# Self attentions of a four-layer decoder: value products regrouped into four 32-column blocks, results gathered by selecting matmuls, TensorE kept in written order

## The chip, the cores and the metric

The kernel runs on one core of one Trainium2 chip. The metric is the device time of the whole program in microseconds (us). Three runs of the kernel before took 5355.73, 5357.63 and 5362.43 us; the median is 5357.63 us. About 0.2% (some 11 us) is what a measurement of this kernel can tell from no change.

## The reference, cut to what matters

The model is a decoder of four layers on 16 batches of 100 tokens with 128 features, all in float32. Each layer is a self attention, a cross attention to 1444 context rows and a feed-forward part, each with a residual. Only the four self attentions are changed. All have 16 heads of 8 features (q, k), and 100 queries against 100 keys:

```python
# layer 0 (scores / 0.1, values times a gate), layer 1 (plain), both causal
scores = where(causal, einsum('bhqd,bhkd->bhqk', q, k) * scale, -inf)
out = einsum('bhqk,bhkd->bhqd', softmax(scores), v) ; x += out @ w_out.T
# layer 2, not causal: two attention maps over values of 16 features per head
att = softmax(q1 @ k1) - lam * softmax(q2 @ k2)
y = einsum('bhts,bhse->bhte', att, v); y = rmsnorm(y) * ... ; x += y @ c_w.T
# layer 3, causal: q and k normed, scores clipped before the softmax
scores = where(causal, clip(q @ k * scale, -5, 5), -10000); attn = softmax(scores / 1.5)
```

## The kernel before, in words

`run` calls twelve stages one after the other; each begins with a layer norm of `X` (100 tokens on the partitions, 16 batches x 128 features), so a stage can't begin before the one before it has written its last batch of `X`. The stages that the change touches are `l0_attn`, `l1_attn`, `l2_attn` and `l3_attn`.

A self attention first norms and turns `X`, then projects `qT` and `kT` (features on the partitions, `project`) and values per batch (`ps_v`) into `va`, a tile of 9 columns per head: 8 values and a column of ones, whose product gives the softmax's sum (17 columns in layer 2). Then it loops over units: one batch in layers 0, 1 and 3, and one batch of one of the two maps in layer 2, so 16, 16, 32 and 16 units. One unit is:

- `attn_scores`: GpSimd spreads the keys into `kb` (each head's 8 rows kept, the others zero, L287). Four matmuls of 400 columns (L298) give the scores of 16 heads in PSUM. VectorE adds the mask or clips (L305, L307), or VectorE and ScalarE copy (L311), into `sc`. VectorE takes the row maxima `mx` (L313), GpSimd subtracts them (L314), ScalarE takes the exponential (L315).
- `attn_pv`: 16 transposes (L328) in four groups of four, each group into one of two PSUM banks of `psT`, evacuated by `copy`, which takes VectorE and ScalarE in turn (L247, L249). Then 16 matmuls (L333), one per head: the turned numerators are the weights (100x100) and 9 or 17 columns of values move. VectorE takes the reciprocal of the sums, `rs` (L335).
- `o` (L419) is the normed result; `attn_out` turns it (`ps_ot`, L344), copies it (`ot`, L346), multiplies it with the output weights (`ps_out`, L349) and adds it to `X` (L351). In layer 2 this comes after the loop, for 16 batches.

The scores of unit b+1 are written ahead of the transposes of unit b. The order on each engine is not the written one: a planner orders the instructions of each engine by when it reckons them ready, with the written order as priority. An instruction that goes through `tc.keep_in_program_order` is tied behind the one written before it on its engine. `l0_xattn` and `l2_xattn` tie all their matmuls in this way; the self attentions tie none. [...] in a self attention `psS` has two tiles of two banks, `psT` two of one, `psO` two of one. Every float32 matmul appears in the trace as two weight loads and two passes.

`l2_xattn` already multiplies values in the way that the change brings to the self attentions: 32 value columns as weights, four such blocks side by side in TensorE's columns (`ps_O`, L1018), then four matmuls with a constant of zeros and ones, `so`, that pick the heads' columns out (`ps_o`, L1051).

Of the kernel before, what the change touches and what calls it, by code (L numbers as in the profile page):

```python
# [9 lines left out]
F32 = mybir.dt.float32  # L10
U8 = mybir.dt.uint8
AF = mybir.ActivationFunctionType
# [20 lines left out]
def _pack(parts, axis):  # L33

    at, n = {}, 0
    for name, a in parts:
        at[name] = (n, a.shape[axis])
        n += a.shape[axis]
    return np.ascontiguousarray(np.concatenate([a for _, a in parts], axis=axis)), at


def _layout(i):
# [54 lines left out]
        ("ident", (p == q)), ("hmask", p // 8 == np.arange(NH)[None, :]), ("tri", tri), ("tri3", tri3),  # L97
# [50 lines left out]
    hm, so = np.zeros((4, 32, 4), f), np.zeros((4, 32, 4, NH, 9), f)  # L148
    uk, uv = up(i["L2_xattn_wk"], i["L2_xattn_bk"]), up(i["L2_xattn_wv"], i["L2_xattn_bv"])
    for r in range(4):  # L150
        for a in range(4):
            blk, o, h = (0, 9 * a, 3 * r + a) if a < 3 else (1, 0, 12 + r)
            d = slice(8 * h, 8 * h + 8)
            qa[:, blk, r, o : o + 8] = i["L2_xattn_wq"][:, d]
            qb[32 * r + o : 32 * r + o + 8, blk, 0] = i["L2_xattn_bq"][d]
            ka[:, blk, r, o : o + 8], va[:, blk, r, o : o + 8] = uk[:, d], uv[:, d]
            ka[CD, blk, r, o + 8] = va[CD, blk, r, o + 8] = 1.0
            hm[r, o : o + 8, a], hm[r, o + 8, a] = 1.0 / math.sqrt(8.0), 1.0
            so[r, o + np.arange(9), a, h, np.arange(9)] = 1.0
    arr["l2x"], xat["l2x"] = _pack([  # L160
        ("q", qa.reshape(128, 256)), ("bq", qb.reshape(128, 2)), ("hm", hm.reshape(128, 4)),
        ("so", so.reshape(128, 576)), ("wo", i["L2_xattn_wo"])], 1)
# [22 lines left out]
class Decoder:  # L185
# [97 lines left out]
    def attn_scores(self, b, wp, psS, qT, kT, mask, mode):  # L283

        nc = self.nc
        kb = wp.tile([128, NH, S], F32, tag="kb", name="kb")
        nc.gpsimd.tensor_tensor(  # L287
            kb,
            kT[:, b * S : (b + 1) * S].unsqueeze(1).to_broadcast([128, NH, S]),
            self.k("hmask").unsqueeze(2).to_broadcast([128, NH, S]),  # L290
            ALU.mult,
        )
        sc = wp.tile([S, NH, S], F32, tag="sc", name="sc")
        for g in range(2):
            ps = psS.tile([128, 2, 512], F32, tag="s", name="ps_s")
            for j in range(2):
                h = 8 * g + 4 * j
                nc.tensor.matmul(  # L298
                    ps[:S, j, :G4], lhsT=qT[:, b * S : (b + 1) * S],
                    rhs=kb[:, h : h + 4, :].rearrange("p h k -> p (h k)"), start=True, stop=True,  # L300
                )
                src = ps[:S, j, :G4].rearrange("p (h k) -> p h k", k=S)
                dst = sc[:, h : h + 4, :]
                if mode == "add":
                    nc.vector.tensor_tensor(dst, src, mask.unsqueeze(1).to_broadcast([S, 4, S]), ALU.add)  # L305
                elif mode == "clip":
                    nc.vector.scalar_tensor_tensor(  # L307
                        dst, src, -5.0, mask.unsqueeze(1).to_broadcast([S, 4, S]), ALU.max, ALU.min
                    )
                else:  # L310
                    self.copy(dst, src)  # L311
        mx = wp.tile([S, NH], F32, tag="mx", name="mx")
        nc.vector.tensor_reduce(mx, sc, AX.X, ALU.max)  # L313
        nc.gpsimd.tensor_tensor(sc, sc, mx.unsqueeze(2).to_broadcast([S, NH, S]), ALU.subtract)  # L314
        nc.scalar.activation(  # L315
            sc.rearrange("p h k -> p (h k)"), sc.rearrange("p h k -> p (h k)"), AF.Exp,
            scale=(1.0 / 1.5 if mode == "clip" else 1.0),
        )
        return sc

    def attn_pv(self, wp, psT, psO, sc, va, dv):

        nc = self.nc
        pt = wp.tile([S, NH, S], F32, tag="pt", name="pt")
        for g in range(4):
            ps = psT.tile([128, 512], F32, tag="ps", name="ps_pt")
            for j in range(4):
                nc.tensor.transpose(ps[:S, j * S : (j + 1) * S], sc[:, 4 * g + j, :], self.ident[:S, :S])  # L328
            self.copy(pt[:, 4 * g : 4 * g + 4, :].rearrange("p h k -> p (h k)"), ps[:S, :G4])
        po = psO.tile([128, 512], F32, tag="po", name="ps_pv")  # L330
        pv = po[:S, : NH * (dv + 1)].rearrange("p (h e) -> p h e", h=NH)
        for h in range(NH):
            nc.tensor.matmul(pv[:, h, :], lhsT=pt[:, h, :], rhs=va[:, h, :], start=True, stop=True)  # L333
        rs = wp.tile([S, NH], F32, tag="rs", name="rs")
        nc.vector.reciprocal(rs, pv[:, :, dv])  # L335
        return pv, rs
# [30 lines left out]
    def attn_pools(self, st):  # L367
# [3 lines left out]
        psS = st.enter_context(tc.tile_pool(name="psS", bufs=2, space=PSUM))  # L371
        psT = st.enter_context(tc.tile_pool(name="psT", bufs=2, space=PSUM))
        psO = st.enter_context(tc.tile_pool(name="psO", bufs=2, space=PSUM))
        return wp, w1, psS, psT, psO

    def l0_attn(self):
        nc = self.nc
        with ExitStack() as st:
            wp, w1, psS, psT, psO = self.attn_pools(st)
# [11 lines left out]
            va = w1.tile([S, B, NH, 9], F32, name="va")  # L391
            nc.gpsimd.memset(va[:, :, :, 8:9], 1.0)
# [15 lines left out]
            self.attn_loop(wp, psS, psT, psO, qT, kT, self.k("tri")[:S], "add", va, self.w("l0_out"), 0.1)  # L408

    def attn_loop(self, wp, psS, psT, psO, qT, kT, mask, mode, va, wo, scale):  # L410
        nc = self.nc
        nxt = self.attn_scores(0, wp, psS, qT, kT, mask, mode)
        for b in range(B):
            sc = nxt
            if b + 1 < B:
                nxt = self.attn_scores(b + 1, wp, psS, qT, kT, mask, mode)
            pv, rs = self.attn_pv(wp, psT, psO, sc, va[:, b], 8)
            o = wp.tile([S, NH, 8], F32, tag="o", name="o")
            nc.vector.tensor_tensor(o, pv[:, :, 0:8], rs.unsqueeze(2).to_broadcast([S, NH, 8]), ALU.mult)  # L419
            self.attn_out(b, wp, psT, psO, o.rearrange("p h e -> p (h e)"), wo, scale)  # L420
# [22 lines left out]
    def l1_attn(self):  # L443
        nc = self.nc
        with ExitStack() as st:
            wp, w1, psS, psT, psO = self.attn_pools(st)
# [8 lines left out]
            va = w1.tile([S, B, NH, 9], F32, name="va")  # L455
            nc.gpsimd.memset(va[:, :, :, 8:9], 1.0)
# [5 lines left out]
            self.attn_loop(wp, psS, psT, psO, qT, kT, self.k("tri")[:S], "add", va, wo, 1.0)  # L462

    def l2_attn(self):
        nc = self.nc
        with ExitStack() as st:
            wp, w1, psS, psT, psO = self.attn_pools(st)
# [17 lines left out]
            t = []  # L485
            for j in range(4):
                d = w1.tile([128, NT], F32, name=f"qk{j}")
                self.project(psT, self.w("l2_qk", 128 * j, 128), XT, d, None, 1.0 / math.sqrt(8.0) if j < 2 else 1.0)
                t.append(d)
            va = w1.tile([S, B, NH, 17], F32, name="va")  # L490
            nc.gpsimd.memset(va[:, :, :, 16:17], 1.0)
            for b in range(B):
# [3 lines left out]
                self.copy(va[:, b, :, 0:16], ps[:S, :256].rearrange("p (h e) -> p h e", h=NH))  # L496
# [13 lines left out]
            Y = va[:, :, :, 0:16]  # L510
            ss = w1.tile([S, B, NH], F32, name="ss")

            def scores(u):
                b, j = divmod(u, 2)
                return self.attn_scores(b, wp, psS, t[j], t[2 + j], None, "none")

            nxt = scores(0)
            for u in range(2 * B):
                b, j = divmod(u, 2)
                sc = nxt  # L520
                if u + 1 < 2 * B:
                    nxt = scores(u + 1)
                pv, rs = self.attn_pv(wp, psT, psO, sc, va[:, b], 16)
                if j == 0:
                    y1 = wp.tile([S, NH, 16], F32, tag="y1", name="y1")
                    nc.vector.tensor_tensor(y1, pv[:, :, 0:16], rs.unsqueeze(2).to_broadcast([S, NH, 16]), ALU.mult)
                    continue
                y = Y[:, b]
                nc.vector.tensor_scalar(rs, rs, nlam, None, ALU.mult)
                y2 = wp.tile([S, NH, 16], F32, tag="y2", name="y2")  # L530
                nc.vector.tensor_tensor(y2, pv[:, :, 0:16], rs.unsqueeze(2).to_broadcast([S, NH, 16]), ALU.mult)
                nc.gpsimd.tensor_tensor(y, y1, y2, ALU.add)
                sq = wp.tile([S, NH, 16], F32, tag="sq", name="sq")
                nc.gpsimd.tensor_tensor(sq, y, y, ALU.mult)
                nc.vector.tensor_reduce(ss[:, b, :], sq, AX.X, ALU.add)
            nc.scalar.activation(ss, ss, AF.Sqrt, bias=self.eps[1e-5][:S], scale=1.0 / 16.0)
# [10 lines left out]
    def l3_attn(self):  # L547
        nc = self.nc
        with ExitStack() as st:
            wp, w1, psS, psT, psO = self.attn_pools(st)  # L550
# [6 lines left out]
            va = w1.tile([S, B, NH, 9], F32, name="va")  # L557
            nc.gpsimd.memset(va[:, :, :, 8:9], 1.0)
# [28 lines left out]
            self.attn_loop(wp, psS, psT, psO, qkT[0], qkT[1], self.k("tri3")[:S], "clip", va, self.w("l3_out"), 0.5)  # L587
# [295 lines left out]
    def l2_xattn(self):  # L883
# [13 lines left out]
        with ExitStack() as st:  # L897
# [147 lines left out]
            def after(b):  # L1045
# [4 lines left out]
                for a in range(4):  # L1050
                    mm(ps[:S, :144], lhsT=os[:, a * S : (a + 1) * S], rhs=w("so")[:, 144 * a : 144 * a + 144],  # L1051
# [595 lines left out]
```

## Time and profile before

| | |
|---|---|
| median of three runs | 5357.63 us |
| the profiled execution | 5356.96 us, span 5355.2 us, mean granted TensorE clock 0.85 |
| busy | PE 80%, weight loads 50%, DVE 67%, ACT 36%, POOL 18% |
| `l0_attn`, first score matmul to last `X` | 55.6 to 211.2 us |
| `l1_attn`, the same | 1816.5 to 1977.6 us |
| `l2_attn`, to the last sum of squares (L535) | 2319.9 to 2607.1 us |
| `l3_attn`, to the last `X` | 3675.1 to 3837.0 us |

PE is TensorE's matmuls and PEld its weight loads, DVE VectorE, ACT ScalarE, POOL GpSimd, SP the queue of most transfers. A line of a view has the start in us, the time taken in us, the engine, the line of the kernel, the operation, the tile written and the tiles read, the shape, the number of instructions, and in brackets how long the engine had been idle and what ended that. PEclk is TensorE's granted clock: 1.00 is full, 0.50 half.

### The profile page before, as it was taken

Reading aid. Unit: us, or ns where it says so; the run is one execution under the profiler, and the core shown is the slowest. Engines: PE = TensorE matmul, PEld = TensorE weight load, DVE = VectorE, ACT = ScalarE, POOL = GpSimd, SP = SyncE. Lnnn points to the kernel's source line nnn. Section 1 sums busy time; section 2 is a strip of 40 time slices with the busy share of each in tenths; the row PEclk is TensorE's granted clock in tenths of the full one; section 3 lists DMA queues with packets and bytes.
Section 4 is the critical chain, followed back from the end, with each engine's and each line's share of the span. In section 5 each row is a group of like instructions: output and inputs, shape, how many; then the busy total and the mean of one; then the engine's idle time right before and its main releaser. Section 6 shows DMA issues by size and latency. Waiting matters only on the chain.

```text
span 5355.2 us, 62956 instructions
## 1 busy us (share of the span) xinstructions
PE 4291.5 (80%) x24304; PEld 2652.9 (50%) x24304; DVE 3593.9 (67%) x6846; ACT 1938.0 (36%) x3660; POOL 987.7 (18%) x671
## 2 busy tenths in 40 slices
PE   6999999999999887989899999977733334331599
PEld 4655555555567665556545655554511112111377
DVE  5577777777743465445457767635699999997533
ACT  2366666666622232233224554531222222221222
POOL 6300000000000352067400000016411121111200
PEclk9799999999999879889669999986766666655699
DMA  2100000000000013000000000000100000000000
GB/s 53 69 14 14 17 18 13 14 18 14 1 1 1 2 44 109 1 2 1 14 9 14 10 14 14 6 1 1 69 22 17 17 17 20 19 4 0 1 4 4
DMA packets 17618, 91.60 MB, mean 17 GB/s; under 512 B 2428, under 2 KB 2909, under 8 KB 16130
## 3 DMA queue, kind: packets, MB, share of 16 engines
q1 hardware_dynamic: 16954, 86.62, 5.3%
q8 instruction: 192, 3.15, 0.2%
q10 hardware_dynamic: 364, 0.96, 0.1%
q14 instruction: 108, 0.88, 0.1%
HBM read 86.74 MB, written 0.82 MB: 16 GB/s over the span
## 4 chain that ended last, share of the span: by engine, by line
PE 67%; DVE 24%; POOL 6%; issue 2%; ACT 1%; DMA 0%; POOLq 0%; ACTq 0%; DVEq 0%
PE ps_o L766 10%; PE ps_s L766 10%; DVE m L1482 7%; DVE wk L1483 7%; PE ps_s L913 5%; PE ps_o L1196 4%; PE ps_pv L333 4%; PE ps_s L298 4%; PE pg L1210 3%; PE pu L1212 3%; PE ps_O L913 3%; PE ps_st L913 3%; PE ps_k L913 2%; PE ps_v L913 2%; DVE y L1567 2%
## 5 line engine op out<-in xcount | busy, mean ns | idle before, releaser
L766 PE MATMUL ps_s<-qk,ct 97*128 97x400 f32 (+1 forms) x1536 | 650.9, 506 | 0.7 <-DVE qk L796 0.7
L1476 PE MATMUL ps_s<-ct,qk 97*100 97x512 f32 (+1 forms) x384 | 254.9, 816 | 493.2 <-ACT ex L1488 492.5
L766 PE MATMUL ps_o<-st,cn 128*97 128x400 f32 (+1 forms) x1536 | 649.7, 505 | 0.4 <-ACT st L834 0.4
L1004 DVE TENSOR_REDUCE pm<-ps_s 100x1 f32<-100x484 f32 (+1 forms) x768 | 470.4, 654 | 258.8 <-PE ps_s L913 258.8
L803 ACT COPY st<-ps_s 128x400 f32<-128x400 f32 (+1 forms) x768 | 375.5, 489 | 424.1 <-PE ps_s L766 420.5
L812 DVE TENSOR_TENSOR mx<-mx,st 128x400 f32<-128x400 f32 (+1 forms) x640 | 365.3, 571 | 172.4 <-ACT st L803 168.8
L1038 ACT ACTIVATE pt<-ps_st 121x400 f32<-121x400 f32 (+1 forms) x768 | 345.0, 501 | 366.8 <-PE ps_s L913 342.3
L913 PE MATMUL ps_s<-K,q 32*100 32x484 f32 (+1 forms) x1536 | 439.0, 641 | 7.4 <-DVE pm L1004 7.4
L833 DVE TENSOR_TENSOR st<-st,nb 128x400 f32<-128x400 f32 (+1 forms) x768 | 403.6, 567 | 8.6 <-ACT nb L829 2.5
L834 ACT ACTIVATE st<-st 128x400 f32<-128x400 f32 (+1 forms) x768 | 377.8, 535 | 41.1 <-DVE st L833 41.0
L1476 PEld LDWEIGHTS ps_s<-ct,qk 97*100 97x100 f32 x384 | 83.4, 237 | 623.9 <-ACT ex L1488 518.4
L913 PE MATMUL ps_st<-q,K 32*121 32x300 f32 (+3 forms) x3072 | 381.2, 360 | 7.4 <-ACT pt L1038 7.4
L766 PEld LDWEIGHTS ps_s<-qk,ct 97*128 97x128 f32 (+1 forms) x1536 | 266.9, 184 | 234.1 <-issue 90.0
L766 PEld LDWEIGHTS ps_o<-st,cn 128*97 128x97 f32 (+1 forms) x1536 | 237.1, 163 | 234.3 <-issue 142.6
L1483 DVE MATCH_REPLACE8 wk<-m,wk 100x1444 f32<-100x1444 f32 x192 | 315.0, 1645 | 0.0
L1482 DVE MAX8 m<-wk 100x8 f32<-100x1444 f32 x192 | 311.7, 1651 | 0.0
L913 PEld LDWEIGHTS ps_st<-q,K 32*121 32x121 f32 (+1 forms) x3072 | 272.1, 180 | 56.0 <-ACT pt L1038 9.6
L333 PEld LDWEIGHTS ps_pv<-va,pt 100*100 100x100 f32 x2560 | 266.2, 183 | 38.9 <-DVE pt L247 18.8
L1488 ACT ACTIVATE ex<-ps_s,nm 100x1444 f32<-100x1444 f32 x64 | 93.7, 1463 | 521.7 <-DVE nm L1486 506.2
L1215 ACT ACTIVATE sl<-pg 128x400 f32<-128x400 f32 x256 | 128.8, 503 | 424.0 <-PE pg L1210 265.0
L333 PE MATMUL ps_pv<-va,pt 100*100 100x9 f32 (+1 forms) x2560 | 265.5, 244 | 14.5 <-DVE pt L247 9.5
L822 POOL TENSOR_TENSOR nd<-cst_sb,nm 100x400 f32<-100x400 f32 x64 | 54.6, 853 | 1182.8 <-DVE nm L820 1182.8
(457 smaller groups left out, 7821.0 us busy)
## 6 DMA issues: line engine op xcount, KB each, us to landing
ct<-in_ctxT SPq DMA_DIRECT2D x64, 541.5 KB
cn<-in_ctxn SPq DMA_DIRECT2D x48, 582.0 KB
l0f_sb<-in_l0f SPq DMA_DIRECT2D x3, 2048.0 KB
l3f_sb<-in_l3f SPq DMA_DIRECT2D x3, 2048.0 KB
wts_sb<-in_wts SPq DMA_DIRECT2D x1, 2576.5 KB
l0x_raw<-in_l0x SPq DMA_DIRECT2D x1, 1800.0 KB
l1f_sb<-in_l1f SPq DMA_DIRECT2D x1, 1728.0 KB
X<-in_x SPq DMA_DIRECT2D x1, 800.0 KB
```

The costliest lines, as they stand in the source:

```text
L333: nc.tensor.matmul(pv[:, h, :], lhsT=pt[:, h, :], rhs=va[:, h, :], start=True, stop=True)
L766: mm = lambda *a, **k: tc.keep_in_program_order(nc.tensor.matmul(*a, **k))
L803: nc.scalar.copy(t[:n], ps[:n, :G4])
L812: nc.vector.tensor_tensor(MX[u][:n], MX[u][:n], t[:n], ALU.max)
L833: nc.vector.tensor_tensor(t[:n], t[:n], NM[u][:n], ALU.subtract)
L834: nc.scalar.activation(t[:n], t[:n], AF.Exp)
L913: mm = lambda *a, **k: tc.keep_in_program_order(nc.tensor.matmul(*a, **k))
L1004: nc.vector.tensor_reduce(pm[:, a, r // 32, n : n + 1], ps[:S, : n1 - n0], AX.X, ALU.max)
L1038: nc.scalar.activation(pt[: n1 - n0, r // 32, :], ps[: n1 - n0, :G4], AF.Exp)
L1476: nc.tensor.matmul(ps[:S, n0:n1], lhsT=qk[:, h, :], rhs=ct[:, n0:n1], start=True, stop=True)
L1482: nc.vector.max(m8[:, j, :], cur)
L1483: nc.vector.match_replace(wk, m8[:, j, :], cur, MARK)
```

## The change

`attn_scores`, `attn_pv` and the loops are replaced by one function, `attn`, for all four layers.

- The values lie in `va` with 9 columns per head (two halves of 8 values in layer 2, each with its ones: 288 columns), and 24 spare columns. The whole tile is set to 1.0 (`spread`) before the values are written.
- The turned numerators move, and 32 columns of values (three heads and what follows them, or one head) are the weights. A unit takes eight matmuls of 300 or 100 columns, four column blocks each, into one bank (16 in layer 2: two banks). ScalarE copies the bank to `os`.
- Four matmuls (eight in layer 2) with the constant `so` pick each head's columns out of `os` and bring the queries back to the partitions. `so` moves from `l2x` to the constants `cst`.
- All matmuls and transposes of a loop are tied in written order. The step of the loop at `i` writes: scores of `i`, results of `i-4`, transposes of `i-2`, the turn of `o` of `i-5`, values of `i-3`, the output product of `i-5`. Other engines are ordered by the planner as before.
- `psS` has three tiles of one bank, `psO` three, `psT` two as before; `sc` has three buffers.
- In layer 3 the row maxima and their subtraction are left out: its scores are clipped.
- In layer 2 the four q and k tiles lie in the shared buffer `big`, and the values are copied in two halves.

```diff
-        sc = wp.tile([S, NH, S], F32, tag="sc", name="sc")
...
-        mx = wp.tile([S, NH], F32, tag="mx", name="mx")
-        nc.vector.tensor_reduce(mx, sc, AX.X, ALU.max)
-        nc.gpsimd.tensor_tensor(sc, sc, mx.unsqueeze(2).to_broadcast([S, NH, S]), ALU.subtract)
...
-        for h in range(NH):
-            nc.tensor.matmul(pv[:, h, :], lhsT=pt[:, h, :], rhs=va[:, h, :], start=True, stop=True)
-        rs = wp.tile([S, NH], F32, tag="rs", name="rs")
-        nc.vector.reciprocal(rs, pv[:, :, dv])
...
+    def attn(self, pools, units, halves, mode, finish):
+        pin = tc.keep_in_program_order
+        mm = lambda *a, **k: pin(nc.tensor.matmul(*a, **k))
+        turn = lambda o, i: pin(nc.tensor.transpose(o, i, self.ident[: i.shape[0], : i.shape[0]]))
...
+        def scores(i):
...
+            sc = scs[i] = wp.tile([S, NH, S], F32, tag="sc", name="sc", bufs=3)
+            for h in range(0, NH, 4):
+                ps = psS.tile([128, 512], F32, tag="s", name="ps_s")
+                mm(ps[:S, :G4], lhsT=q[:, cols], rhs=kb[:, h : h + 4, :].rearrange("p h k -> p (h k)"), start=True, stop=True)
...
+            if mode != "clip":
+                mx = wp.tile([S, NH], F32, tag="mx", name="mx")
+                nc.vector.tensor_reduce(mx, sc, AX.X, ALU.max)
+                nc.gpsimd.tensor_tensor(sc, sc, mx.unsqueeze(2).to_broadcast([S, NH, S]), ALU.subtract)
...
+        def turned(i):
...
+            for g in range(4):
+                ps = psT.tile([128, 512], F32, tag="ps", name="ps_pt")
+                for j in range(4):
+                    turn(ps[:S, j * S : (j + 1) * S], sc[:, 4 * g + j, :])
+                self.copy(pt[:, g * G4 : (g + 1) * G4], ps[:S, :G4])
+
+        def values(i):
+            pt, va = pts.pop(i), units[i][3]
+            oss[i] = []
+            for k in range(halves):
+                ps = psO.tile([128, 512], F32, tag="po", name="ps_pv")
+                for blk in range(2):
+                    for r in range(4):
+                        c0, n = (3 * r * S, 3 * S) if blk == 0 else ((12 + r) * S, S)
+                        at = 144 * k + 9 * (3 * r if blk == 0 else 12 + r)
+                        mm(ps[32 * r : 32 * r + 32, 3 * S * blk : 3 * S * blk + n], lhsT=va[:, at : at + 32],
+                           rhs=pt[:, c0 : c0 + n], start=True, stop=True)
+                os = wp.tile([128, G4], F32, tag=f"os{k}", name="os")
+                nc.scalar.copy(os, ps[:, :G4])
+                oss[i].append(os)
+
+        def results(i):
+            ps = psO.tile([128, 512], F32, tag="po", name="ps_so")
+            for k, os in enumerate(oss.pop(i)):
+                for a in range(4):
+                    mm(ps[:S, 144 * k : 144 * k + 144], lhsT=os[:, a * S : (a + 1) * S], rhs=so[:, 144 * a : 144 * a + 144],
+                       start=a == 0, stop=a == 3)
...
+            nc.vector.reciprocal(rs, v[:, 0, :, 8])
+            fin[i] = finish(i, v, rs, mm, turn)
+            next(fin[i], None)
+
+        for i in range(N + 6):
+            for lag, step in ((0, scores), (4, results), (2, turned), (5, lambda j: next(fin[j], None)), (3, values),
+                              (5, lambda j: next(fin[j], None))):
+                if 0 <= i - lag < N:
+                    step(i - lag)
...
-        psS = st.enter_context(tc.tile_pool(name="psS", bufs=2, space=PSUM))
+        psS = st.enter_context(tc.tile_pool(name="psS", bufs=3, space=PSUM))
         psT = st.enter_context(tc.tile_pool(name="psT", bufs=2, space=PSUM))
-        psO = st.enter_context(tc.tile_pool(name="psO", bufs=2, space=PSUM))
+        psO = st.enter_context(tc.tile_pool(name="psO", bufs=3, space=PSUM))
...
-            va = w1.tile([S, B, NH, 9], F32, name="va")
-            nc.gpsimd.memset(va[:, :, :, 8:9], 1.0)
+            vs, (va,) = self.spread(pools)
```

## The prediction

> **What bounds the kernel now.** I read the page first, its 40 slices: busy tenths and granted clock.
>
> ```profile
> PE   6999999999999887989899999977733334331599
> ...
> PEclk9799999999999879889669999986766666655699
> ```
>
> A slice is 134 us. TensorE is nearly full, and in the slices of the self attentions (2, 14, 15, 18, 28, 29) its clock is below full, while in slices 3 to 13, the first cross attention, it is full. Next, the chain of waits from 40 to 215 us (start, time taken, what).
>
> ```profile
> by line: PE ps_pv L333 26.1%; PE ps_s L298 25.8%; PE ps_pt L328 9.8%; DVE mx L313 7.2%; PE ps_proj L358 3.8%; POOL xn L264 3.7%; POOL sc L314 3.3%; DVE sc L305 2.3%; DVE pt L247 2.3%; PE ps_w L604 2.2%; ACT sc L315 1.8%; PE ps_out L349 1.7%
> ...
> 100.56 2.75 PE ps_pv L333 x32
> ...
> 117.67 2.75 PE ps_pv L333 x32
> ```
>
> The chain runs through TensorE's value products and scores, and repeats after 17.11 us, so 8.55 us per unit. Layer 1 has 8.4 to 8.55, layer 3 8.56 (kb from 3672.2 to 3800.6 in 15 steps), layer 2 8.28 (2314 to 2570.7 in 31). VectorE is busy 65% from 60 to 190 us, TensorE 95%. The timeline of TensorE tells what the 8.55 are made of (start, time, out<-in, shapes, count):
>
> ```profile
> 117.50 2.91 PE L333 MATMUL ps_pv<-va,pt 100*100 100x9 f32 x32
> 120.27 2.88 PE L298 MATMUL ps_s<-kb,qT 128*100 128x400 f32 x4
> ...
> 127.83 1.50 PE L333 MATMUL ps_pv<-va,pt 100*100 100x9 f32 x16
> 129.18 1.84 PE L298 MATMUL ps_s<-kb,qT 128*100 128x400 f32 x4
> ```
>
> Starts give the pass: 32 value passes 2.77 (87 ns each for 9 columns: weight loads set it). Four score passes take 2.67 us in the second line and 1.68 or less in the fourth. The windows say why (stretch, length, busy PE, PEld, DVE, ACT, POOL, granted clock):
>
> ```profile
> 119.50:120.00 0.50, 0.50 (x8) 0.50 (x8) 0.00 (x0) 0.22 (x1) 0.25 (x1) 1.00 0.00 0
> 120.50:121.00 0.50, 0.50 (x2) 0.12 (x2) 0.47 (x2) 0.50 (x1) 0.00 (x0) 0.50 0.00 0
> 124.00:124.50 0.50, 0.50 (x7) 0.50 (x6) 0.50 (x2) 0.00 (x0) 0.50 (x1) 1.00 0.00 0
> ```
>
> From 120.4 to 123.8, and again from 137.4 to 140.8, the clock is half, each time after a whole run of 32 value passes. The halves of 16 with scores between (125.7 to 129.2) bring no drop. One drop of 3.4 us in two units costs 1.7 us, 0.85 per unit. So a unit holds about 7.2 us of full-clock work (scores 2.68, 16 transposes 1.4, values 2.75, small ones 0.35), 0.85 of slow clock, 0.5 of waits.
>
> **The change part by part.** *Values.* Out go 32 passes, 2.75 us. In come eight column-block matmuls and four selecting ones; `l2_xattn` has both shapes (its PE and weight rows):
>
> ```profile
> 3003.09 0.88 PE L913 MATMUL ps_O<-pt,V 121*32 121x300 f32 x16
> ...
> 3011.52 0.74 PE L913 MATMUL ps_o<-l2x_sb,os 128*100 128x144 f32 x4
> ```
>
> Values cost 0.88 plus 0.19 us of entering (the weight row there has 0.20 idle of PE's own issue, median of its 184 entries) and about as much on leaving; the selecting matmuls 0.12 per pass, 8 passes 0.96. Bounds: 1.7 (latencies overlap) and 2.3 (both gaps, every time); I take 2.2. So a unit is 2.68+0.96+1.4+0.87+0.31+0.2 = 6.4 us against 7.2; layer 2 has two halves, 2×0.96+2.68+1.4+0.19+1.33 = 7.5 against 7.1. The blocks running in turn rather than beside each other would be 2.0 per unit more; the row excludes it.
>
> The Trainium skill, "TensorEngine Tiling (Array Packing)", Key Properties, says that a change of tiling mode drains TensorE. The row's price for it is the 0.2 above: 80 units at 0.19 and 0.17, some 29 us, already in the sums; the rule gives no other figure, so both lead to the same total unless the drain also waits for results, 0.17 more per unit or 14 us.
>
> *Order.* TensorE now takes a written order: scores of i, results of i-4, transposes of i-2, turn of o, values of i-3, output product. Before, the planner filled a gap with whatever was ready; now a late copy stops all. Where is one late? VectorE's timeline of before:
>
> ```profile
> 148.78 1.82 DVE L313 TENSOR_REDUCE mx<-sc 100x16 f32<-100x1600 f32 x1
> 150.51 0.28 DVE L351 SCALAR_TENSOR_TENSOR X<-ps_out,X 100x128 f32<-100x128 f32 x1
> 150.71 0.56 DVE L247 COPY pt<-ps_pt 100x400 f32<-100x400 f32 x1
> ```
>
> The maxima run ahead of the copy that frees a transpose bank. Taken over to the new order, from the first score pass: scores 0 to 2.68, the last mask add (0.57) to 3.45, maxima to 5.27, reciprocal and `o` to 5.82. TensorE: results to 3.64, transpose groups 1 and 2 to 4.34; group 3 when ScalarE has copied group 2, 5.15 to 5.5; group 4 when VectorE has copied group 1 (5.82 to 6.38), 6.43 to 6.78; VectorE's copy of group 3 to 6.95, so the turn of `o` 7.0 to 7.1, values to 8.15, output to 8.4. So 8.4 us, of which 2 are waits: the time won in the values is lost to `pt`. Behind the waiting group 4 stand in TensorE's order the turn of `o`, the values, the output product and the next scores, so ScalarE's next `os`, the addition to `X` and the next unit's mask all come that much later. If the maxima gave way, 6.5; if bank rotation fell worst, 9.0.
>
> *Clock.* The drops of the long value runs go. From 3.64 to 7.1 only transposes and waits remain, 3.46 us against a slow stretch of 3.4 us; I charge one drop in four units, 0.4. That gives 8.8 in layers 0 and 1. Bounds 0 and 1.7.
>
> *Layer 3.* Maxima (1.82 x16 on VectorE) and subtraction (2.86 x16 on GpSimd) go. VectorE has then 4.3 us per unit and is in time for the copies; 6.4 plus about 1.1 of waits for copies and POOL's kb gives 7.4 to 7.6. Bounds 6.5 and 8.8.
>
> *Layer 2.* Scores are copied, half by ScalarE, so VectorE is less late: 7.5 plus 0.85 of waits for copies plus 0.4 of clock gives 8.75, against 8.28. Bounds 7.85 and 10.2.
>
> *Hidden.* The fill of `va`, 2688 or 4992 columns, at POOL's 0.311 us per 100x256: 3.3 us, in layer 2 6.1; POOL is idle 299 us before 1800.57 and 139 before 2293.11. In layer 0 the gates (16 x0.6 from 71 us) already set the start. Uncovered all four are 16 us. 112 `os` copies (0.50) lie on ScalarE, 36% busy; uncovered 56 us, partly counted in the range. The second half of layer 2's value copies, 16 more of some 0.25, lies ahead of the first pinned score: 2 us, in its start. The `so` constant, 288 KB, moves forward into the first load: at the 142 GB/s of the first 50 us 2 us; the mask lands at 24.24 and gates VectorE, so +1.5, bounds 0 and 2.1. The queues of SP and POOL issue no more DMAs than before. `l3x_raw` (112 KB, issued 2289.94) now waits for the shared buffer until layer 2's end, 2610; it is needed at 3837.
>
> *Stages, first score to end.* Between loops nothing changes. Steps 0 to 2 end when the first unit has gone through mask, maxima, subtraction (2.86), exponential (1.54) and transposes, 12.5 after its scores; step 3 has no results yet, 7.5; then full periods, 12 (28 in layer 2); then six emptying steps. Layer 0: the gates hold the start, fourth step ended at 89.2, twelve periods 105.6, emptying 15: 209.8 against 211.2, -1.4. Layer 1: 1818.5+12.5+7.6+105.6+15 = 1959.2 against 1977.6, -18.4. Layer 2: 2324.7+12.5+7.3+28×8.75+20.5 = 2610 against 2607.1, +3. Layer 3: 3675+19+12×7.6+14 = 3799 against 3837, -38. Sum -55, with the constant -53.
>
> That is 5356.96 (the profiled execution; span 5355.2 and 1.8 around it) less 53: 5304. The median, 5357.63, is 0.7 more, within its own spread.
>
> **A rule against it.** Layer 3's start, in windows of a microsecond:
>
> ```profile
> 3687.00:3688.00 1.00, 0.00 (x0) 0.00 (x0) 0.74 (x1) 1.00 (x1) 1.00 (x1) 1.00 0.00 0
> 3689.00:3690.00 1.00, 0.68 (x9) 0.65 (x9) 0.35 (x2) 0.49 (x1) 1.00 (x2) 1.00 0.00 0
> 3691.00:3692.00 1.00, 1.00 (x8) 1.00 (x7) 0.48 (x1) 0.00 (x0) 1.00 (x1) 0.50 0.00 0
> ```
>
> After waiting and transposes the clock drops at 3690.6. The skill, "TensorE: Matmul & The Clock Gate", Part 4, says that transposes do not count as TensorE busy. Then the new stretch of transposes and waits is as good as idle, and each unit may drop, 1.7 us. The rule in the same page that idle gaps over about 3 us bring the drop (the table at its end) would charge nothing, as the old drops came with TensorE busy throughout and the new gaps are 0.8 at most. The trace is nearer to the first; 3.46 against 3.4 us is why I charge a quarter.
>
> **Rivals.** (A) Slower: the clock drops in every unit of layers 0 to 2 after the transposes. That is 1.3 more than I charge: 52 full periods 68, some 9 filling and emptying steps 11, so 5304+79 = 5383. For it: the rule and the stretch; against it: 0.9 us of values and 1 us of results at either side stream wide. It decides where 53 us are spent on these 61 steps, 0.87 each: from three units in four dropping. (B) Faster: copies precede the maxima, TensorE never waits, 6.5, 7.85 and 6.5 us: twelve or 28 periods shorter, layer 0 -29, layer 1 -46, layer 2 -22, layer 3 -51, so about 5210. The next late thing would be POOL, with kb and subtraction 5.72 a unit. For it: TensorE's order is fixed, so copies become ready at other times than before; against it: the row at 148.78. (C) No change: A in just three units of four, layer 3's gain lost again in layer 2, about 5357. (D) Blocks in turn: 5490.
>
> **How the numbers follow.** Main case 0.61, 5304, own range 5272 to 5337; A 0.22; B 0.10; C 0.05; D 0.02. About 0.2% is what a measurement can tell from no change. Faster: main and B, with 0.01 of A at its low end, 0.72; same 0.05; slower 0.23. The range leaves B's far end and D out: 5230 to 5390.
>
> **What would show it.** PEclk in the loops at 1.00 in most units and 0.50 in a quarter; PE waiting for `pt` from VectorE before group 4, with maxima just before; value groups of 16 passes at 0.88 and selecting ones near 1.0; layer 3 at 7.4 to 7.6 us a unit, and the ends of the four stages 1, 20, 17 and 55 us earlier than before (less the 1.5). A period of 10 us at 0.50 is A; a period of 6.5 is B; wrong for a reason I don't list if a first score waits, for the fill or for the last value copy.

## The result, and the profile after

The changed kernel takes 5429.52 us (median of four runs, 5428.13 to 5431.95) against 5358.27 for the kernel before: ratio 1.0133, 95% interval 1.0115 to 1.015. It is slower by 71 us, where 53 us less were forecast, and the time lies outside the range. The profiled execution has a span of 5426.6 us. Its slices of busy tenths and granted clock:

```profile
PE   4799999999999877888879999996833333431499
...
PEclk9799999999999978899959999997955666555699
```

The spans of the stages, from the first score matmul to the last `X` (layer 2: to the last sum of squares), read from the two timelines:

| us | before | forecast, change | after | change |
|---|---|---|---|---|
| layer 0 | 155.6 | -1.4 | 202.4 | +46.8 |
| layer 1 | 161.1 | -18.4 | 193.5 | +32.4 |
| layer 2 | 287.2 | +3 | 305.1 | +17.9 |
| layer 3 | 161.9 | -38 | 128.1 | -33.8 |
| all else | | +1.5 | | +8.1 |

The changes sum to the +71.4 of the spans. Of the 8.1, 4.0 lie ahead of the first score (59.60 instead of 55.63). Layer 3 went nearly as forecast; layers 0 and 1 did not. Their steady step, in TensorE's timeline (the stretch that answers to the lines at 117 to 131 us of before; the bracket is idle time and what ended it):

```profile
171.99 0.31 PE L301 MATMUL ps_ot<-cst_sb,o 100*128 100x100 f32 x1
172.23 0.89 PE L300 MATMUL ps_pv<-pt,va 100*32 100x300 f32 x16
175.72 0.75 PE L300 MATMUL ps_out<-wts_sb,ot 128*100 128x128 f32 x2 [2.60 <-ACT ot L391]
176.26 5.48 PE L300 MATMUL ps_s<-kb,qT 128*100 128x400 f32 x8
...
185.59 0.31 PE L301 MATMUL ps_ot<-cst_sb,o 100*128 100x100 f32 x1
...
189.32 0.75 PE L300 MATMUL ps_out<-wts_sb,ot 128*100 128x128 f32 x2 [2.61 <-ACT ot L391]
```

The period is 189.32 - 175.72 = 13.6 us, not 8.8. The values take 0.89 us as forecast. Then TensorE waits 2.6 us for `ot`, although the turn of `o` ended at 172.30; and the eight score passes take 5.48 us, about twice the 2.85 us that they take at full clock. The list of waits (engine, what waits, for what: us in total, times, longest) has it ten times between 110 and 240 us:

```profile
PE ps_out L300 <- ACT ot L391: 25.8, 10, 2.6
```

ScalarE's timeline, and GpSimd's, say what the `ot` ahead of 189.32 waited for (its turn of `o` ended at 185.90):

```profile
187.60 1.54 ACT L329 ACTIVATE sc<-sc 100x1600 f32<-100x1600 f32 x1 [1.60 <-POOL sc L327]
189.05 0.22 ACT L391 COPY ot<-ps_ot 128x100 f32<-128x100 f32 x1
189.17 0.49 ACT L352 COPY os<-ps_pv 128x400 f32<-128x400 f32 x1
```
```profile
181.88 2.87 POOL L310 TENSOR_TENSOR kb<-kT,cst_sb 128x1600 f32<-128x1600 f32 x1 [7.92 <-PE ps_s L300]
184.71 2.86 POOL L327 TENSOR_TENSOR sc<-sc,mx 100x1600 f32<-100x1600 f32 x1
```

On ScalarE the exponential of the step stands ahead of `ot`. That exponential belongs to the scores at 176.26: it needs their mask, maxima and subtraction. TensorE's written order has the output product ahead of the next scores. So each step is one closed chain: scores, mask, maxima, subtraction, exponential, `ot`, output product, next scores. The subtraction itself starts when GpSimd has spread the next keys (`kb`, to 184.75), 0.5 us after the maxima, which ended at 184.27. ScalarE is idle for 1.60 us in front of the exponential, with the operand of `ot` ready. And the clock (stretch, length, busy PE, PEld, DVE, ACT, POOL, granted clock, DMA, GB/s):

```profile
119.00:120.00 1.00, 0.92 (x17) 0.42 (x16) 0.00 (x0) 0.21 (x1) 1.00 (x1) 1.00 0.00 0
120.00:121.00 1.00, 0.00 (x0) 0.00 (x0) 0.00 (x0) 0.19 (x1) 0.78 (x1) 0.55 0.00 0
...
124.00:125.00 1.00, 1.00 (x2) 0.32 (x2) 0.28 (x1) 0.00 (x0) 0.00 (x0) 0.50 0.00 0
...
126.00:127.00 1.00, 1.00 (x2) 0.32 (x2) 0.56 (x1) 0.00 (x0) 0.00 (x0) 0.53 0.00 0
127.00:128.00 1.00, 1.00 (x6) 0.65 (x5) 0.69 (x2) 0.00 (x0) 0.01 (x1) 1.00 0.00 0
```

It is half from 120.1 (0.55 is the mean of that microsecond) to 126.9, through the wait and the scores. It falls 0.2 us after the value passes ended, so what TensorE did before, transposes with short waits and 0.9 us of values, has a share in the fall; the wait alone can't have brought it. Longer scores lengthen the chain, so the period grew from 12.15 (110.38 to 122.53) to 13.64. There it stayed, with 6.83 us at half clock and 6.83 at full clock in turn from 120.1 on. Layer 3 has the same written order, but its exponential needs no maxima and no subtraction. TensorE's timeline, then ScalarE's:

```profile
3834.49 0.89 PE L300 MATMUL ps_pv<-pt,va 100*32 100x300 f32 x16
3835.30 0.46 PE L300 MATMUL ps_out<-wts_sb,ot 128*100 128x128 f32 x2
3835.60 2.85 PE L300 MATMUL ps_s<-kb,qkT 128*100 128x400 f32 x8
...
3843.16 2.85 PE L300 MATMUL ps_s<-kb,qkT 128*100 128x400 f32 x8
```
```profile
3839.09 1.54 ACT L329 ACTIVATE sc<-sc 100x1600 f32<-100x1600 f32 x1 [3.11 <-DVE sc L321]
...
3842.20 0.24 ACT L391 COPY ot<-ps_ot 128x100 f32<-128x100 f32 x1
```

The exponential starts 3.5 us after the first score of its step and is over long before `ot`. There is no wait for `ot`, the scores are at full clock, and the period is 7.56.

### The profile page after: what moved, and what is told of

The parts are those of the page before. It is cut to its first block, busy times and chain, and to the rows that moved or that the text cites. A ratio compares the mean times of both kernels' runs of the same rounds, so it can differ in the third digit from the quotient of the medians.

```text
span 5426.6 us, 63295 instructions
## 1 busy us (share of the span) xinstructions
PE 4250.7 (78%) x24432; PEld 2555.4 (47%) x24432; DVE 3609.0 (67%) x6838; ACT 1977.2 (36%) x3779; POOL 951.8 (18%) x655
## 4 chain that ended last, share of the span: by engine, by line
PE 62%; DVE 23%; POOL 9%; issue 3%; ACT 2%; DMA 0%; ACTq 0%; POOLq 0%; DVEq 0%
PE ps_s L813 10%; PE ps_o L813 10%; DVE m L1529 7%; DVE wk L1530 7%; PE ps_s L960 5%; PE ps_o L1243 4%; PE pg L1257 3%; PE pu L1259 3%; PE ps_s L300 3%; PE ps_O L960 3%; PE ps_st L960 3%; POOL sc L327 2%; PE ps_k L960 2%; PE ps_v L960 2%; DVE y L1614 2%
## 5 line engine op out<-in xcount | busy, mean ns | idle before, releaser
L1263 DVE TENSOR_TENSOR h<-sl,pu 128x400 f32<-128x400 f32 x256 | 146.2, 571 | 160.0 <-PE pu L1259 159.4
L1547 POOL TENSOR_TENSOR AM<-AM,ex 100x1444 f32<-100x1444 f32 x48 | 155.0, 3229 | 455.6 <-ACT ex L1546 455.5
```

## The experiments

Beside the runs below, the kernel before took 5359.35 to 5363.21 us, against 5358.27 beside the changed kernel. So a difference of 5 us between runs measured at different times can hardly be told from none, nor can a few microseconds of a stage's span, which is read from one execution.

Theory: TensorE's written order and ScalarE's order don't fit each other; the wait for `ot` and the half clock that follows are the whole loss of layers 0 and 1. Rivals: the stretch of transposes lowers the clock by itself (rival A of the prediction); ScalarE's copies are too slow; the regrouped work is slower, whatever its order.

**ot_dve**: the copy moved to another engine.

```diff
-            nc.scalar.copy(ot, ps[:, :S])
+            nc.vector.tensor_copy(ot, ps[:, :S])
```

> VectorE copies the turned o (ot) in layers 0, 1 and 3 instead of ScalarE; all else as in the changed kernel. Theory (ScalarE's order: ot stands behind the exponential of the same step, so TensorE waits 2.6 us for it and its clock then drops): the wait before ps_out goes, the granted clock stays at 1.00, the period of layers 0 and 1 falls from 12 to 13.6 us to about 8.4, layer 3 stays at 7.56; 5335 to 5350 us. Rival (the stretch of transposes and bank waits lowers the clock by itself): the clock still drops in every unit, period 10 or more, about 5380. Rival (VectorE becomes the bound, because ot lands behind maxima or mask): period over 9, 5355 or more.

5337.12 us, ratio 0.9961 (0.9947 to 0.9976): 92 us below the changed kernel, and 0.4% below the kernel before. Of the 93 us between the two traces' spans, 43 are in layer 0 and 45 in layer 1; 6 are in layer 2, which the edit does not touch. TensorE's timeline:

```profile
116.19 0.89 PE L300 MATMUL ps_pv<-pt,va 100*32 100x300 f32 x16
117.00 0.46 PE L300 MATMUL ps_out<-wts_sb,ot 128*100 128x128 f32 x2
117.30 2.85 PE L300 MATMUL ps_s<-kb,qT 128*100 128x400 f32 x8
...
125.35 2.85 PE L300 MATMUL ps_s<-kb,qT 128*100 128x400 f32 x8
```

The wait is gone and the period 8.05 where the clock is full. It is not always: of 22 groups of eight score passes in the two layers (from the sixth step on), 8 take 3.66 to 4.51 us, 0.44 us per unit on the mean; with the other passes that fall into the half clock, the mean period of these steps is 8.7. So the clock still falls without the wait, but in some of the steps only, and that is not the main loss. Layer 0 now spans 159.8, layer 1 148.9.

**exp_pin**: the copy stays on ScalarE; the exponential is tied to the end of its step, in all four layers.

```diff
+        def exps(i):
+            flat = scs[i].rearrange("p h k -> p (h k)")
+            pin(nc.scalar.activation(flat, flat, AF.Exp, ...))
...
-                              (5, lambda j: next(fin[j], None))):
+                              (5, lambda j: next(fin[j], None)), (0, exps)):
```

> The exponential of a step is written last in its step and tied behind what stands before it on ScalarE, so ot and os come first; engines and work as in the changed kernel. Theory (only the place of ot behind the exponential costs): as with ot on VectorE, period of layers 0 and 1 about 8.4, 5335 to 5350 us. Rival (ScalarE is slow to copy ot for another reason): the 2.6 us before ps_out stay, about 5430.

5326.52 us, 0.9944 (0.9928 to 0.9961), 8.5 below the expected band; layers 0 and 1 span 157.2 and 148.3.

```profile
116.62 0.55 PE L301 MATMUL ps_pt<-cst_sb,sc 100*100 100x100 f32 x4 [0.33 <-DVE pt L255]
117.29 0.30 PE L301 MATMUL ps_ot<-cst_sb,o 100*128 100x100 f32 x1
117.53 0.88 PE L300 MATMUL ps_pv<-pt,va 100*32 100x300 f32 x16
118.34 0.75 PE L300 MATMUL ps_out<-wts_sb,ot 128*100 128x128 f32 x2
118.88 4.26 PE L300 MATMUL ps_s<-kb,qT 128*100 128x400 f32 x8
```

The wait is gone with the copy on ScalarE. Its place behind the exponential was the cost, not the engine. This step shows as well that the clock can fall without any wait for `ot`: it is half for 3.41 us from 118.3, at the end of the values, and the scores take 4.26.

**fill**: the wait stays, and TensorE streams through it.

```diff
+            if mode == "add":
+                for _ in range(4):
+                    mm(pr[:S, :G4], lhsT=qT[:, :S], rhs=kT[:, :G4], start=True, stop=True)
             mm(pr[:S, :D], lhsT=ot, rhs=wo, start=True, stop=True)
```

> ScalarE's order as in the changed kernel; in layers 0, 1 and 3 four 128x400 matmuls (2.7 us at full clock) that nothing reads stand in TensorE's order ahead of each output product, so TensorE streams while it waits for ot. Theory (the idle 2.6 us bring the half clock of the next scores): the clock stays at 1.00, scores take 2.85 instead of 5.5 us, the period of layers 0 and 1 falls to about 11 although TensorE does more, layer 3 rises by 2.7 a unit (+38); together about 5430 - 25 + 38 = 5443. Rival (the drop comes from the transposes' stretch, or the clock plays no part): the period of layers 0 and 1 stays at 13.6 or rises.

In the kernel the extra matmuls are in layers 0 and 1 alone, so the +38 for layer 3 falls away, and the theory's sum is 5405. Measured: 5396.36 (two runs), 1.0072 (1.0052 to 1.0092), 33 below the changed kernel with more work on TensorE.

```profile
173.82 2.93 PE L300 MATMUL ps_out<-kT,qT 128*100 128x400 f32 x8
176.59 0.38 PE L300 MATMUL ps_out<-wts_sb,ot 128*100 128x128 f32 x2
176.81 2.85 PE L300 MATMUL ps_s<-kb,qT 128*100 128x400 f32 x8
```

The period is 176.81 - 166.07 = 10.74 (the scores before began at 166.07). The scores take 2.85 us again; a drop of 3.41 us is left in two or three of the last ten steps of each layer, which then take 12.4 (one has its extra matmuls at 4.60 us). So of the 5.55 us between 13.6 and 8.05, about half (2.9) is half clock that goes when the wait is filled, and the rest (2.7) is the wait itself, now spent on the extra matmuls. With the wait the clock is half in every step, for 6.83 us; with the wait filled (here) or gone (ot_dve, exp_pin), in some steps and nearly always for 3.41 us.

**out_late**: only the place of the output product in TensorE's written order moves.

```diff
-        for i in range(N + 6):
-            for lag, step in ((0, scores), (4, results), ..., (3, values),
-                              (5, lambda j: next(fin[j], None))):
+        for i in range(N + 7):
+            for lag, step in ((0, scores), (6, lambda j: next(fin[j], None)), (4, results), ..., (3, values)):
```

> The changed kernel with one place moved in TensorE's written order: the output product of a unit stands behind the scores of the next step (lag 6) instead of ahead of them; every engine's work, and ScalarE's order with ot behind the exponential, stay. Theory (TensorE's order and ScalarE's order do not fit each other, neither is slow by itself): the exponential is over while TensorE runs scores, so the 2.6 us go; period of layers 0 and 1 about 8.05 with half-clock scores in a third of the units, 5325 to 5345 us. Rival (the chain of a step, scores to exponential, 9.7 us, sets the period wherever ot is used, since os stands behind the exponential as well): period 9.5 or more, 5365 or more.

5320.58 us, 0.9924 (0.9908 to 0.9941). TensorE's timeline, then ScalarE's:

```profile
132.67 0.88 PE L300 MATMUL ps_pv<-pt,va 100*32 100x300 f32 x16
133.48 2.93 PE L300 MATMUL ps_s<-kb,qT 128*100 128x400 f32 x8
136.25 0.38 PE L300 MATMUL ps_out<-wts_sb,ot 128*100 128x128 f32 x2
```
```profile
134.38 1.54 ACT L329 ACTIVATE sc<-sc 100x1600 f32<-100x1600 f32 x1 [1.60 <-POOL sc L327]
135.83 0.22 ACT L391 COPY ot<-ps_ot 128x100 f32<-128x100 f32 x1
```

ScalarE's order is as it was: exponential, then `ot`, 1.60 us idle in front. But TensorE is at its scores meanwhile; the period is 7.84 (the next scores begin at 141.32), and the clock full from 96 to 192 us, most of layer 0's loop. exp_pin moved ScalarE's order alone and out_late TensorE's alone, and each removes the wait: the loss lay in the two together.

**unpin**: the ties on TensorE's order are taken away.

```diff
-        pin = tc.keep_in_program_order
+        pin = lambda x: x
```

> The changed kernel with the ties on TensorE's order taken away: matmuls and transposes are ordered by the planner, with the written order as priority. Theory (the wait for ot is a matter of two orders that do not fit each other, TensorE's written one and ScalarE's planned one): with both planned, ot comes before the exponential, no wait of 2.6 us, 5310 to 5350. Rival (the new work itself is slower, order aside): 5400 or more.

5292.2 us, 0.9863 (0.9847 to 0.988): better than expected. The changed work is faster than the old one; 137 of the changed kernel's microseconds come from the written order. But the 71 us gained on the kernel before are not all the regrouping's: layer 3, which has lost its maxima and subtraction too, is 48 shorter (113.8), layers 0 and 1 are 8.5 and 21.5 shorter (147.1, 139.6), and layer 2 is 11 longer (298.1). No run has the maxima left out without the regrouping.

```profile
132.87 0.25 PE L301 MATMUL ps_ot<-cst_sb,o 100*128 100x100 f32 x1
132.96 1.51 PE L300 MATMUL ps_s<-kb,qT 128*100 128x400 f32 x4
135.12 0.46 PE L300 MATMUL ps_out<-wts_sb,ot 128*100 128x128 f32 x2 [0.66 <-ACT ot L391]
```

The expectation, `ot` ahead of the exponential, did not come true: here too `ot` is copied behind one. But the planner put four score passes between the turn of `o` and the output product; 0.66 us of wait is left, and score passes lie among the transposes, so the stretch without them is short (clock 0.99 from 100 to 190 us). Layer 3 spans 113.8 us, 14 below the written order: its period is 6.65.

**mx_late**: VectorE's maxima tied behind the transposes' copies, the exponential tied behind the next scores.

```diff
+                pin(nc.vector.tensor_reduce(mx, sc, AX.X, ALU.max))
...
+            for lag, step in ((0, scores), (1, exps), (4, results), (2, turned), (0, maxima), (5, ...),
+                              (3, values), (5, ...)):
```

> In all layers VectorE's row maxima of a step are written after the transposes of that step and tied behind their copies; the exponential of a step is written after the scores of the next step and tied behind what stands before it on ScalarE. Same work as in the changed kernel. Theory (what is left of waits in layers 0 and 1 is the copy of pt behind the maxima, and the long stretch of transposes that this makes brings the remaining half clock): copies take 0.3 to 0.6 us of wait as in layer 3, the period of layers 0 and 1 falls from about 8.8 to about 7.5, layer 2 from 8.9 to 8.2; 5275 to 5290 us. Rival (bank rotation of the transposes sets the wait, whatever VectorE's order): periods unchanged, within 5 us of 5326.

5304.27 us, 0.9889 (0.9874 to 0.9903). In layers 0 and 1 it is as expected:

```profile
122.30 2.85 PE L300 MATMUL ps_s<-kb,qT 128*100 128x400 f32 x8
124.98 1.14 PE L300 MATMUL ps_so<-cst_sb,os 128*100 128x144 f32 x8
125.96 0.85 PE L301 MATMUL ps_pt<-cst_sb,sc 100*100 100x100 f32 x8
127.28 0.89 PE L301 MATMUL ps_pt<-cst_sb,sc 100*100 100x100 f32 x8 [0.47 <-DVE pt L255]
...
129.85 2.85 PE L300 MATMUL ps_s<-kb,qT 128*100 128x400 f32 x8
```

Period 7.55, clock 1.00 from 100 to 190 us, layers 0 and 1 at 144.4 and 135.3. It is the period of layer 3, which has no maxima: behind the copies they cost nothing that shows. (The edit moves the exponential as well; exp_pin, which moves it alone, has 8.05 at full clock.) Layer 2 did not follow: 298.5 us, a period of 9.05 where 8.2 had been expected. That part of the expectation failed, and the total is 14 above the expected band.

**l2_stt** and **mx_stt**: what holds layer 2. VectorE's timeline of the changed kernel, then GpSimd's:

```profile
2520.99 0.51 DVE L255 COPY pt<-ps_pt 100x400 f32<-100x400 f32 x1
2521.42 2.46 DVE L572 TENSOR_SCALAR rs<-rs,nlam 100x16 f32<-100x16 f32 x1
2523.91 0.42 DVE L573 TENSOR_TENSOR y<-ps_so,rs 100x256 f32<-100x256 f32 x1
```
```profile
2520.99 2.86 POOL L327 TENSOR_TENSOR sc<-sc,mx 100x1600 f32<-100x1600 f32 x1
```

Sixteen elements take 2.46 us, and end at 2523.88, with GpSimd's subtraction (2523.85). Before, the same product took 0.22 us, while GpSimd was idle:

```profile
2466.80 0.22 DVE L529 TENSOR_SCALAR rs<-rs,nlam 100x16 f32<-100x16 f32 x1
```

The edit folds it into the products that write `y2`:

```diff
-                nc.vector.tensor_scalar(rs, rs, nlam, None, ALU.mult)
-                nc.vector.tensor_tensor(y2, w, r4, ALU.mult)
+                r3 = rs.unsqueeze(2).to_broadcast([S, NH, 8])
+                for k in range(2):
+                    nc.vector.scalar_tensor_tensor(y2[:, :, k], v[:, k, :, 0:8], nlam, r3, ALU.mult, ALU.mult)
```

> Only layer 2: the product of rs and lambda (16 elements, 2.46 us each, ends with GpSimd's subtraction) is folded into the two products that write y2 for the second map. Theory (that multiplication is held until GpSimd's operation ends, and the transposes' copy stands behind it): the period of layer 2 falls from 8.99 by 0.4 to 0.7, 10 to 20 us in all, 5410 to 5420. Rival (TensorE waits for its banks in any order): within 3 us of 5430.

5419.46 us, 1.0115 (1.01 to 1.013): 10 below the changed kernel. In layer 2 two steps together take 17.37 us instead of 17.98, which is 9.8 in 16 pairs, and the layer spans 293.2. In its VectorE timeline the two products together take 0.6 us:

```profile
2468.24 0.59 DVE L574 SCALAR_TENSOR_TENSOR y<-ps_so,nlam,rs 100x128 f32<-100x128 f32 x2
2468.97 0.57 DVE L255 COPY pt<-ps_pt 100x400 f32<-100x400 f32 x1
```

The Trainium skill, "SBUF — State Buffer", section "Who interferes with whom", says that such a product on VectorE can exclude, and be excluded by, an operation of GpSimd, for the whole length of the one that came first. The two end times agree with that, and so does mx_late: there the product falls behind GpSimd's `kb` instead, and takes 1.14 us, to its end.

> As mx_late, and in layer 2 the product with lambda folded into the two products that write y2. Theory: 5 to 10 us less than mx_late, as VectorE is no longer held by GpSimd's operation ahead of the copies. Rival: same as mx_late within 3 us, since with the maxima later the multiplication does not meet GpSimd's subtraction.

5298.58 us, 0.9879 (0.9864 to 0.9894), 5.7 below mx_late; the runs of the two overlap at the edge, so the sign is likely and the size rough. Layer 2 at 294.1. The rival had supposed that the product no longer meets an operation of GpSimd; it met `kb`.

**l2_old**: mx_late with layer 2 as it was before.

> As mx_late, with layer 2 as in the kernel before (values as moving operand, planner's order). Theory: layer 2 takes 287 us again; if mx_late brings the new layer 2 to 8.2 a unit (about 275 us), this is 10 us or so slower than mx_late; if its new layer 2 stays at 299, this is 12 faster.

5289.19 us, 0.9859 (0.9845 to 0.9874), 15 below mx_late, with layer 2 at 287.8: the second case of the expectation. In layer 2 the regrouping does not pay in any of these orders. The likely reason, not tested apart: two halves double the column blocks and the selecting matmuls (1.55 and 2.14 us a unit at full clock, from 2703.40 to 2707.09 in the changed kernel, 3.7 together), against passes of 17 columns that cost no more than passes of 9 (16 of them 1.51 us at 2486.80 in the kernel before, 1.50 in layer 0), 2.7 us a unit.

**best**: l2_old, with layer 3 in the planner's order.

```diff
-        pin = tc.keep_in_program_order
+        pin = tc.keep_in_program_order if mode == "add" else lambda x: x
```

> Layers 0 and 1 as in mx_late (written orders on TensorE, VectorE's maxima and ScalarE's exponential), layer 3 with the planner's order, layer 2 as in the kernel before. Theory (stage times add up): layers 0, 1 and 2 as in l2_old, layer 3 114 instead of 126 us, so 5276. Rival (layer 3's planned order depends on what stands before it): 5289 as l2_old.

5278.28 us, 0.9844 (0.9829 to 0.9859): the stage times add up, and this beats both kernels, the one before by 1.6%.

## Why the prediction was wrong, point by point

- **The step that failed** is the end of the timetable, "so the turn of `o` 7.0 to 7.1, values to 8.15, output to 8.4". It lets the copy `ot` (0.22 us) pass under the values, as if it cost nothing. The timetable follows TensorE and VectorE; of ScalarE it has one copy of `pt`, and elsewhere the prediction says only that ScalarE is "36% busy". The exponential of the step was never placed. It starts 8.8 us after the first score even at full clock (out_late: 133.48 to 142.28), and stands ahead of `ot`. So the output product, put at 8.15 to 8.4, could not start before about 10.5 us, and the period came to 13.6 with the half clock. A busy share says nothing of what stands ahead in an engine's order. The miss is 48 us in layer 0 and 51 in layer 1, out of 125; without the wait (ot_dve) 43 and 45 of these are gone.
- **The new waits.** I asked what stands behind a late copy of `pt` (right, and it was late: 0.64 and 0.33 us per step, less than the 2 charged). I did not ask the same of `ot`, which lies between two pinned products of TensorE and goes through ScalarE. "The new gaps are 0.8 at most" failed here: the new gap was 2.6.
- **The clock.** Charged were 0.4 us per unit for a stretch of transposes near 3.4 us. Where `ot` does not wait, the charge was of the right kind and somewhat small: in ot_dve the scores alone lose 0.44 per unit, and the mean period is 8.7 instead of 8.05. That this is near the forecast 8.8 is in part luck, as the waits were put too high and the clock too low. Rival A's form came true in the changed kernel (half clock in every step of layers 0 and 1 once steady), but at a size that A did not have, and not by the transposes alone: fill shows that the idle 2.6 us are needed for it. In layer 2's steady steps there were almost no drops: granted clock 0.99 from 2420 to 2680 us.
- **Values and selecting matmuls.** Right: 0.89 for 16 passes, and 8 passes at 0.98 (181.57 to 182.55 in the changed kernel) against the 0.96 forecast. The sum of 6.4 us holds one of the two gaps around the values (0.2), though both were said to be in it; that is some 0.17 us a unit.
- **The period without the wait**: 8.05 at full clock where 8.4 was worked out, because the last copies waited less. Rival B (copies ahead of the maxima) is a real lever: mx_late has 7.55, not 6.5.
- **Layer 3**: 7.56 against 7.4 to 7.6, and -33.8 against -38. The number was right, the reason in part: VectorE is in time, and TensorE waits 0.66 us a step for its copies. But the gain was put down to the maxima's cost on VectorE. mx_late keeps them in layers 0 and 1 and has the same period, and of the 6.1 us between 13.64 and 7.56 all but 0.5 go with the wait for `ot` (8.05 in ot_dve). What weighed was that here the exponential does not come late.
- **Layer 2**: +17.9 against +3. Its period is 8.99 on the mean (steps of 9.22 and 8.76) against 8.75. The product with lambda, costed at nothing, was held for 2.46 us ahead of a copy that TensorE waits for; l2_stt puts 10 us on it. Another 5.8 us are half clock in the emptying steps, 13.65 us long from 2686.9: ot_dve, fill and out_late, with the same layer 2, span 299.3 there instead of 305.1. What brought it in this execution is open.
- **All else**: +8.1 against +1.5; 4.0 of it before the first score, which stands behind the last value projections now (57.38 to 59.60). The prediction had named such a wait as a sign of being wrong; it was small. The rest was not taken apart.

What stays open: why the planner puts the exponential ahead of `ot` (the traces show the order it chose, not what it reckoned), and how the transposes and the wait share in the fall of the clock.

## What to carry to other kernels

When one engine's order is written by hand and the others' are planned, draw the timetable for every engine that a pinned instruction depends on, the half-idle ones too, and ask of each copy what stands ahead of it in its own queue. Look at the clock after such a wait: here one of 2.6 us was paid about twice, since the matmuls after it ran at half clock. Before a written order is judged by what it computes, run it without the ties: here the whole change of work was worth -1.4%, and the order +2.6% on top of it.

## What the runs showed of the hardware that was not expected

A stretch of transposes, 0.9 us of values and an idle 2.6 us were followed by scores at half clock in every steady step; with the wait filled with matmuls, the scores ran at full clock (fill: 2.85 us in all steady steps). The granted clock has two values in these traces, 1.0 and 0.5, and in all twelve every stretch of one of them lasts a multiple of 3.41 us, but for the one that the end of the program cuts off. The steady period of 13.64 us is four of these; that the loop falls into step with them is what the numbers suggest, not what a run tested. And a product of 16 elements on VectorE can take 2.46 us instead of 0.22 when GpSimd is at work: it ends 0.03 us after GpSimd's operation.
